# Another place for half of the inner sums of a two-level Strassen attention block, and an earlier time for some of them

## The chip, the cores and the metric

The kernel runs on one core of one Trainium2 chip. The metric is the device time of one execution in microseconds, the median of three runs. Lower is better. All data is fp32.

The engines have short names in the profile: PE is TensorE's matmul and PEld its weight load, DVE is VectorE, ACT is ScalarE, POOL is GpSimd (here almost only an issuer of DMAs), and SP is SyncE (the same).

## The reference

An image is 512 channels by 1024 positions; there are 16. Each is group-normalised, projected to q, k and v, attended in four heads of 128 channels, projected back and added to the input.

```python
xn  = groupnorm(x)                                   # (16, 512, 1024), 8 groups
qkv = einsum('oc,bcn->bon', qkv_w, xn) + qkv_b       # 1536 x 512 weights
q, k, v = split(qkv)                                 # four heads of 128
attn = softmax(einsum('bhnd,bhmd->bhnm', q, k) / sqrt(128))
out  = einsum('bhnm,bhmd->bhnd', attn, v)
out  = einsum('oc,bcn->bon', proj_w, out) + proj_b
return x + out
```

## The kernel before

The four projections of an image (first pair of heads' q and k, second pair's, v, and the output projection) are each made by Strassen's method on two levels: seven outer products, in four groups of two, two, two and one (`OUTER`), and in each group seven inner products (`ORDER`). For an outer product the inner level needs four inner sums of the right-hand operand, t1 to t4. VectorE makes them.

```python
OUTER = ((1, 5), (2, 6), (7, 4), (3,))
ORDER = (1, 2, 6, 5, 7, 4, 3)
```

The products are dealt out as units between the matmuls of attention, which run through everything: in each of eight steps of a head there are two score products (`s`, line 741) with their exponentials on ScalarE, and two of the weighted sum (`po`, line 836). The stages of image b are staggered against those of image b + 1:

```python
def plan_head(b, h):
    # h == 0: second pair's q and k of image b; sums of o of image b - 1
    # h == 1: output projection of image b - 1; load and normalise x of image b + 1
    # h == 2: first pair's q and k of image b + 1
    # h == 3: v of image b + 1
```

One function makes all four. Cuts are marked with "# ...".

```python
def two_levels(name, site, b, blocks, finish, sums="make"):
    R = {}
    haves = [{} for _ in OUTER]
    # ...
    def group_units(g):
        # ...
        def sum_tile(h, m):
            haves[h][m] = tpool.tile([P, 2, Q], F32, tag=f"in_{m}", name=f"{name}_{h}_{m}")
            return haves[h][m][:, : len(OUTER[h])]

        def load(h, m):
            if sums == "load" and h < len(OUTER):
                nc.sync.dma_start(sum_tile(h, m), inner_kept[b, h, m])

        def inner_sum(m):
            if sums == "load":
                return
            sum_tile(g, m)
            a, c = {"t1": ("b12", "b11"), "t2": ("b22", "t1"),
                    "t3": ("t2", "b11"), "t4": ("b21", "t2")}[m]
            for i in range(n):
                nc.vector.tensor_sub(have[m][:, i, :], inner(i, a), inner(i, c))   # L522
            if sums == "keep":
                t = dpool.tile([P, n, Q], F32, tag=f"{m}_{g}", bufs=1, name=f"kept_{m}_{g}")
                inner_kept[b, g, m] = t
                nc.gpsimd.dma_start(t, have[m][:, :n])                             # L526
        # ...
        return [
            unit(weights, lambda: inner_sum("t1"), lambda: inner_sum("t2"), p1),
            unit(lambda: inner_sum("t3"), p2), unit(lambda: inner_sum("t4"), p6),
            unit(lambda: load(g + 1, "t2"), p5), unit(lambda: load(g + 1, "t1"), p7),
            unit(lambda: load(g + 1, "t3"), p4),
            unit(lambda: load(g + 1, "t4"), p3, end),
        ]
```

The pool of `in_t1` to `in_t4` has one buffer for each name. So a group's t1 may be written only after the matmuls of the group before it have read theirs and, where the sums are kept, after the store of theirs has landed. The first pair keeps its sums in DRAM (`"keep"`); v of the same image loads them again (`"load"`); the second pair makes them anew (`"make"`), and so does the output projection.

Products gather in two banks of PSUM per name, x and y. An accumulator is evicted between additions: x by copies on ScalarE (line 448), y by additions on VectorE (line 557, into `r`), and the next product for that bank waits for the eviction.

The outer sums of o (the operand of the output projection) lie in six tiles of their own, `ot20` to `ot41`. Their values are made in head 0 at the latest and read in head 1:

```python
def sums_of_b(b, rows=(1, 2), chunks=range(KC)):       # L277: b["t2"], b["t3"], b["t4"]
    # ...
plan[6].append(lambda: o_blocks(b - 1))                # head 0, step 6
plan[6].append(lambda: sums_of_b(ob[b - 1]))
```

The output projection adds the residual x when a result is finished:

```python
def proj_groups(b):
    def finish(which, r, a, c):
        # ...
        t = ypool.tile([P, HALF], F32, tag="y", name=f"y_{b}_{o}_{half}")   # four buffers
        dma = nc.gpsimd.dma_start(t, x[b, ts(o, P), ts(half, HALF)])        # L712
        # ... not before the last eviction of this image's attention
        nc.vector.scalar_tensor_tensor(t, a, projb_sb[:, o : o + 1], t, ALU.add, ALU.add)  # L721
        nc.vector.tensor_add(t, t, c)                                       # L724
        nc.gpsimd.dma_start(out[b, ts(o, P), ts(half, HALF)], t)            # L725
```

v's results are transposed in blocks by VectorE (line 680), go to DRAM and come back into v's layout. The denominators of a finished head are a transpose and a reduction on VectorE (lines 763 and 765) and some small operations.

Each engine runs its queue in order. The order in which a queue's instructions stand is set when the kernel is built, by a scheduler that works from dependencies, and not by the source text alone.

Of the kernel before, what the change touches and what calls it, by code (L numbers as in the profile page):

```python
# [16 lines left out]
P = 128  # L17
# [4 lines left out]
HALF = 512  # L22
# [137 lines left out]
def fast_path(ctx, tc, x, sources, out, consts, flag, dims):  # L160
# [320 lines left out]
        units = {1: p1, 2: p2, 3: p3, 4: p4, 5: p5, 6: p6, 7: p7}  # L481
        return [units[i] for i in ORDER]

    def two_levels(name, site, b, blocks, finish, sums="make"):

# [3 lines left out]
        def part(g, i, row=None):  # L491
            t = R[g][:, i]
            return t if row is None else t[:, row, :]

        def group_units(g):
            group = OUTER[g]
            n = len(group)
            have = haves[g]

            def weights():  # L500
                have["w"] = group_weights(site, g, b == 0 and site in range(PAIRS))

            def sum_tile(h, m):
                haves[h][m] = tpool.tile(
                    [P, 2, Q], F32, tag=f"in_{m}", name=f"{name}_{h}_{m}"
                )
                return haves[h][m][:, : len(OUTER[h])]

            def load(h, m):
                if sums == "load" and h < len(OUTER):  # L510
                    nc.sync.dma_start(sum_tile(h, m), inner_kept[b, h, m])

            def inner_sum(m):
                if sums == "load":
                    return
                sum_tile(g, m)
                a, c = {
                    "t1": ("b12", "b11"), "t2": ("b22", "t1"), "t3": ("t2", "b11"),
                    "t4": ("b21", "t2"),
                }[m]  # L520
                for i in range(n):
                    nc.vector.tensor_sub(have[m][:, i, :], inner(i, a), inner(i, c))  # L522
                if sums == "keep":
                    t = dpool.tile([P, n, Q], F32, tag=f"{m}_{g}", bufs=1, name=f"kept_{m}_{g}")
                    inner_kept[b, g, m] = t
                    nc.gpsimd.dma_start(t, have[m][:, :n])  # L526

            def inner(i, m):
                if m[0] == "t":
                    return have[m][:, i, :]  # L530
                outer = blocks()[FACTORS[group[i]][1]]
                return outer[int(m[1]) - 1][:, ts(int(m[2]) - 1, Q)]

            def mm(acc, j, first):
                an, bn = FACTORS[j]
                t, slot = SLOTS[an]
                for i in range(n):
                    nc.tensor.matmul(  # L538
                        acc[:, ts(i, Q)], have["w"][t][:, i, slot, :], inner(i, bn),
                        start=(first and i == 0), stop=True, skip_group_check=True,  # L540
                    )

            def out_(which, a, c=None):
                row, half = int(which[1]) - 1, int(which[2]) - 1
                if g not in R:
                    R[g] = rpool.tile(
                        [P, 2, 2, HALF], F32, tag=f"r{g % 3}", name=f"{name}_r{g}"
                    )
                dst = R[g][:, :n, row, ts(half, Q)]

                def view(t):
                    return t[:, : n * Q].rearrange("p (i q) -> p i q", q=Q)

                if c is None:
                    nc.scalar.copy(dst, view(a))
                else:
                    nc.vector.tensor_add(dst, view(a), view(c))  # L557

            p1, p2, p6, p5, p7, p4, p3 = strassen(f"{name}_{g}", mm, out_, n * Q)

            def unit(*steps):
                def one():
                    for f in steps:
                        f()
                    for _ in range(min(len(pending), 2 if g == len(OUTER) - 1 else 1)):
                        pending.pop(0)()
                return one

            def end():
                combine(g)  # L570
                if g == len(OUTER) - 1:
                    run(pending)
                    pending.clear()


            return [
                unit(weights, lambda: inner_sum("t1"), lambda: inner_sum("t2"), p1),
                unit(lambda: inner_sum("t3"), p2), unit(lambda: inner_sum("t4"), p6),
                unit(lambda: load(g + 1, "t2"), p5), unit(lambda: load(g + 1, "t1"), p7),
                unit(lambda: load(g + 1, "t3"), p4),  # L580
                unit(lambda: load(g + 1, "t4"), p3, end),
            ]

        def first_loads():
            for m in ("t2", "t1", "t3", "t4"):
                t = tpool.tile([P, 2, Q], F32, tag=f"in_{m}", name=f"{name}_0_{m}")
                haves[0][m] = t
                nc.sync.dma_start(t, inner_kept[b, 0, m])

        pending = []  # L590

# [18 lines left out]
            elif g == 3:  # L610
                done("c12", (1, 0), (3, 0))

        ahead[name] = first_loads
        return [group_units(g) for g in range(len(OUTER))]


    def qk_groups(b, pair):

        def finish(which, r, a, c):
# [7 lines left out]
            )  # L627

        return two_levels(
            f"qk_{b}_{pair}", pair, b, lambda: xb[b], finish, "make" if pair else "keep"  # L630
        )

    def v_units(b, jj):
# [31 lines left out]
    def v_groups(b):  # L665
# [31 lines left out]
                    rows[which].rearrange("(k m) (q e) -> q m k e", m=BLK, q=n)[q],  # L697
                )

        return two_levels(f"v_{b}", "v", b, lambda: xb[b], finish, "load")  # L700

    def v_block(b, h, j):
        v, n = vs[b, h // 2], NB // NH2
# [1 line left out]

    def proj_groups(b):

        def finish(which, r, a, c):
            of, half = int(which[1]) - 1, int(which[2]) - 1
            o = 2 * of + r  # L710
            t = ypool.tile([P, HALF], F32, tag="y", name=f"y_{b}_{o}_{half}")
            dma = nc.gpsimd.dma_start(t, x[b, ts(o, P), ts(half, HALF)])  # L712

            tc.add_manual_dep(
                dma.ins, last_eviction[b].ins.name,
                mybir.DependencyInfo(
                    mybir.DependencyClass.Sync, mybir.DependencyReason.DATA
                ),
                reason="residual",
            )  # L720
            nc.vector.scalar_tensor_tensor(  # L721
                t, a, projb_sb[:, o : o + 1], t, ALU.add, ALU.add
            )
            nc.vector.tensor_add(t, t, c)  # L724
            nc.gpsimd.dma_start(out[b, ts(o, P), ts(half, HALF)], t)  # L725

        return two_levels(f"pp_{b}", "proj", b, lambda: ob[b], finish)


    ps, tot, po, rinv, last_eviction = {}, {}, {}, {}, {}  # L730
# [246 lines left out]
    def plan_head(b, h):  # L977
# [41 lines left out]
        else:  # L1019

            spread(plan, staggered(next_v.pop()), 0, NB - 1)
        return plan

    def warm(n, name):
# [24 lines left out]
    stage_sums(0)  # L1049
    run(staggered(qk_groups(0, 0)))  # L1050
    next_v, next_qk = [], [qk_groups(0, 1)]
    stage_blocks(1)
    stage_sums(1)

    plan = []
    for s in range(steps + 1):
        units = []
        if s < steps:
# [1 line left out]
            if j == 0:  # L1060
                plan = plan_head(b, h)
            units = plan[j]
            if j == NB - 1 and h > 1 and b + 1 < B:
                (next_v if h == 2 else next_qk).append(
                    v_groups(b + 1) if h == 2 else qk_groups(b + 1, 1)
                )
                if h == 2:
                    units.append(ahead[f"v_{b + 1}"])
        if 0 < s < steps and s % NB == 0:
            denominators(*where(s - 1)[:2])  # L1070
        for half in range(NH2):
# [148 lines left out]
```

## Time and profile before

| | |
|---|---|
| time, median of 3 runs | 3300.77 us (3296.75 to 3302.75) |
| span of the profiled execution | 3293.0 us |
| PE busy | 3198.6 us, 97% |
| DVE busy | 2639.3 us, 80% |
| ACT busy | 1443.6 us, 44% |
| inner sums on DVE, line 522, 128x256 | about 0.41 us each |
| store of a group's inner sum, from issue to landing | 3.5 us (256 KB, median) |
| load of a residual tile | 4.0 us (256 KB, median) |

A listed matmul overlaps the next one, so the sum of busy time overstates how full TensorE is: the distance from start to start tells more. The view of waits names, for each idle stretch of an engine, the instruction whose end released it; the timeline shows the same in square brackets behind the instruction that waited. An idle stretch of an engine that is not the bound costs nothing by itself.

### The profile page before, as it was taken

How to read it: one execution, taken by the hardware profiler on the slowest of the kernel's cores; microseconds unless marked ns; L12 is line 12 of the kernel's file. 1: busy time of each engine (PE TensorE's matmuls, PEld its weight loads, DVE VectorE, ACT ScalarE, POOL GpSimd, SP SyncE). 2: the span in 40 equal slices, each digit the busy share in tenths (PEclk: the TensorE clock that was granted, in tenths of full speed). 3: DMA queues.
4: the chain of work that ended last, by engine and by line, in shares of the span. 5: the costliest groups of instructions: out<-in, count | busy, mean ns of one | idle time of the engine just before them, and what ended most of it. 6: DMA issues, size and time to landing. Idle time of an engine off the chain costs nothing.

```text
span 3293.0 us, 34096 instructions
## 1 busy us (share of the span) xinstructions
PE 3198.6 (97%) x10474; PEld 2177.7 (66%) x10474; DVE 2639.3 (80%) x4625; ACT 1443.6 (44%) x2709; POOL 525.1 (16%) x938
## 2 busy tenths in 40 slices
PE   8999999999999999999999999999999999999999
PEld 6566666666666666666666666666666666666664
DVE  8878878778787787878888787887878878788684
ACT  2535435344353443534435354353533535344342
POOL 1011121111211112111121201212012120121100
PEclk9999999999999999999999999999999999999999
DMA  6554554545545455454554545546455463554631
GB/s 206 196 189 152 168 182 139 181 137 178 169 150 174 140 170 166 155 169 142 179 168 156 172 130 183 169 148 182 132 174 172 147 200 124 176 160 154 195 122 40
DMA packets 210539, 530.59 MB, mean 161 GB/s; under 512 B 33072, under 2 KB 66096, under 8 KB 210352
## 3 DMA queue, kind: packets, MB, share of 16 engines
q1 hardware_dynamic: 128992, 276.88, 27.2%
q0 software_dynamic: 67392, 216.07, 20.0%
q10 hardware_dynamic: 13968, 35.41, 3.1%
q8 instruction: 87, 1.43, 0.2%
q14 instruction: 100, 0.82, 0.1%
HBM read 389.56 MB, written 138.67 MB: 160 GB/s over the span
## 4 chain that ended last, share of the span: by engine, by line
issue 38%; PE 37%; DVE 11%; DMA 7%; POOL 5%; ACT 0%; POOLq 0%; SPq 0%; DVEq 0%
PE po L836 10%; PE s L741 10%; PE qk_x L538 5%; DMA vd<-vu 4%; POOL kept_t L526 4%; PE qk_y L538 4%; PE pp_x L538 4%; PE pp_y L538 3%; DMA out_y<-y 2%; DVE xt L277 2%; DMA y<-in_x 1%; DVE tot L754 1%; DVE vu L680 1%; DVE part L765 1%; DVE tt L763 1%
## 5 line engine op out<-in xcount | busy, mean ns | idle before, releaser
L836 PE MATMUL po<-p,v 128*128 128x512 f32 x2048 | 1056.6, 598 | 0.0
L741 PE MATMUL s<-qk,qk 128*128 128x512 f32 x2048 | 1052.8, 596 | 3.3 <-ACT p L746 3.2
L746 ACT ACTIVATE p<-s 128x512 f32<-128x512 f32 x1024 | 609.7, 596 | 851.6 <-PE s L741 810.0
L836 PEld LDWEIGHTS po<-p,v 128*128 128x128 f32 x2048 | 603.2, 303 | 328.2 <-issue 209.0
L754 DVE TENSOR_TENSOR tot<-tot,p 128x1024 f32<-128x1024 f32 x385 | 468.5, 1217 | 164.6 <-ACT p L746 162.6
L741 PEld LDWEIGHTS s<-qk,qk 128*128 128x128 f32 x2048 | 388.6, 191 | 106.4 <-issue 40.0
L538 PE MATMUL qk_x<-qk_t,w 128*128 128x256 f32 x1344 | 363.2, 387 | 43.0 <-DVE qk_t L522 38.6
L538 PEld LDWEIGHTS qk_x<-qk_t,w 128*128 128x128 f32 x1344 | 248.5, 191 | 211.9 <-issue 106.5
L448 ACT COPY qk_u<-qk_x 128x512 f32<-128x512 f32 (+1 forms) x256 | 136.1, 532 | 333.7 <-PE qk_x L538 286.7
L526 POOL DMA_DIRECT2D kept_t<-qk_t x256 | 138.3, 540 | 505.6 <-DVE qk_t L522 455.9
L688 POOL DMA_DIRECT2D vd<-vu x120 | 66.2, 552 | 747.5 <-DVE vu L680 745.8
L557 DVE TENSOR_TENSOR qk_r<-qk_y,qk_u 128x512 f32<-128x512 f32 (+1 forms) x256 | 158.3, 618 | 25.8 <-ACT qk_u L448 19.7
L538 PE MATMUL pp_x<-pp_t,w_proj 128*128 128x256 f32 x630 | 170.7, 387 | 6.4 <-ACT pp_p L448 6.4
L538 PE MATMUL v_x<-v_t,w_v 128*128 128x256 f32 x630 | 166.6, 381 | 0.0
L725 POOL DMA_DIRECT2D out_y<-y x120 | 66.2, 552 | 624.2 <-DVE y L724 591.6
L557 DVE TENSOR_TENSOR v_r<-v_y,v_u 128x512 f32<-128x512 f32 (+1 forms) x120 | 74.5, 621 | 112.5 <-ACT v_u L448 82.3
L538 PEld LDWEIGHTS pp_x<-pp_t,w_proj 128*128 128x128 f32 x630 | 113.9, 190 | 76.3 <-issue 22.5
L538 PEld LDWEIGHTS v_x<-v_t,w_v 128*128 128x128 f32 x630 | 118.5, 190 | 53.6 <-issue 23.0
L538 PE MATMUL qk_y<-x,w 128*128 128x256 f32 x512 | 144.4, 384 | 9.4 <-DVE qk_r L557 9.3
L693 POOL DMA_DIRECT2D v<-vd x240 | 139.9, 590 | 79.3 <-issue 67.1
L752 DVE TENSOR_TENSOR tot<-p,p 128x1024 f32<-128x1024 f32 x64 | 78.3, 1223 | 78.4 <-ACT p L746 78.4
L448 ACT COPY v_u<-v_x 128x512 f32<-128x512 f32 (+1 forms) x124 | 66.2, 534 | 165.1 <-PE v_x L538 126.2
(204 smaller groups left out, 4524.8 us busy)
## 6 DMA issues: line engine op xcount, KB each, us to landing
kept_t<-qk_t POOLq DMA_DIRECT2D x192, 256.0 KB, 3.5
w<-kept SPq DMA_DIRECT2D x90, 512.0 KB, 4.0
v_t<-kept_t SPq DMA_DIRECT2D x180, 256.0 KB, 3.0
w<-kept SPq DMA_DIRECT2D x90, 384.0 KB, 3.8
rinv<-row ACTq DMA_DIRECT2D x63, 512.0 KB, 5.5
x<-in_x POOLq DMA_DIRECT2D x60, 512.0 KB, 4.9
vd<-vu POOLq DMA_DIRECT2D x120, 256.0 KB, 3.4
v<-vd POOLq DMA_DIRECT2D x240, 128.0 KB, 4.5
```

The costliest lines, as they stand in the source:

```text
L448: nc.scalar.copy(t[n][:, :width], t["x"][:, :width])
L526: nc.gpsimd.dma_start(t, have[m][:, :n])
L538: nc.tensor.matmul(acc[:, ts(i, Q)], have["w"][t][:, i, slot, :], inner(i, bn), start=(first and i == 0), stop=True, skip_group_check=True,)
L557: nc.vector.tensor_add(dst, view(a), view(c))
L688: nc.gpsimd.dma_start(rows[which][ts(h, P), :], u)
L693: nc.gpsimd.dma_start(vs[b, pair][ts(q, BLK), half].rearrange("m h (k i) j -> m (h k) (i j)", k=n), rows[which].rearrange("(k m) (q e) -> ...
L725: nc.gpsimd.dma_start(out[b, ts(o, P), ts(half, HALF)], t)
L741: nc.tensor.matmul(sc, ks[b, h][:, ts(j, P)], qs[b, h][:, ts(half, HALF)], start=True, stop=True)
L746: nc.scalar.activation(ps[s][:, ts(half, HALF)], sc, AF.Exp, scale=SCALE)
L752: nc.vector.tensor_add(tot[b, h], ps[s - 1], ps[s])
L754: added[b, h, j] = nc.vector.tensor_add(tot[b, h][:, i], tot[b, h][:, i], ps[s][:, i])
L836: nc.tensor.matmul(po[b, h][:, i], v_block(b, h, j), ps[s][:, i], start=(j == 0), stop=(j == NB - 1),)
```

## The change

It has three parts.

1. Groups get one of two homes for their inner sums. Home B is the tiles from before, `in_t1` to `in_t4`. Home A is four of the tiles of o's outer sums: t1 and t2 in `ot20` and `ot21`, t3 and t4 in `ot30` and `ot31`. They are free from the end of the output projection until o's next outer sums. The first pair (from the second image on) and v alternate, "ABAB"; the second pair has "ABBB"; the output projection, whose operand lies there, stays "BBBB". A load now goes ahead to the next group of the same home, and v's second group is loaded when its first begins.
2. The second pair's units are prepared already at the end of head 2 of the image before, and the four inner sums of its first group are made in step 6 of that image's head 3 and no longer in its own first units. For the first image that happens ahead of the attention. The first image no longer stores its first pair's sums, which nothing loads.
3. The residual of a result is loaded when the fourth unit of the group that completes it begins (`prepare`), and not when the result is finished.

No work is added or taken out otherwise; the arithmetic is the same.

```diff
-    def two_levels(name, site, b, blocks, finish, sums="make"):
+    def two_levels(name, site, b, blocks, finish, sums="make", homes="BBBB", prepare=None):
 ...
+        def sum_tile(g, m):
+            k = int(m[1]) - 1
+            tag = f"in_{m}" if homes[g] == "B" else f"ot{2 + k // 2}{k % 2}"
+            t = tpool.tile([P, HALF], F32, tag=tag, name=f"{name}_{g}_{m}")
 ...
-            def load(h, m):
-                if sums == "load" and h < len(OUTER):
+            def load(m):
+                h = homes.find(homes[g], g + 1)
+                if sums == "load" and h > 0:
                     nc.sync.dma_start(sum_tile(h, m), inner_kept[b, h, m])
 
             def inner_sum(m):
 ...
+                if sums != "load" and m not in have:
+                    make_sum(g, m)
 ...
             return [
-                unit(weights, lambda: inner_sum("t1"), lambda: inner_sum("t2"), p1),
+                unit(
+                    weights, lambda: first_sums((1,)) if g == 0 and sums == "load" else None,
+                    lambda: inner_sum("t1"), lambda: inner_sum("t2"), p1,
+                ),
                 unit(lambda: inner_sum("t3"), p2), unit(lambda: inner_sum("t4"), p6),
-                unit(lambda: load(g + 1, "t2"), p5), unit(lambda: load(g + 1, "t1"), p7),
 ...
+                unit(lambda: load("t2"), lambda: ready(g), p5), unit(lambda: load("t1"), p7),
+                unit(lambda: load("t3"), p4), unit(lambda: load("t4"), p3, end),
             ]
 ...
+        def first_sums(groups=(0,)):
+            for g in groups:
+                for m in ("t1", "t2", "t3", "t4"):
+                    if sums == "load":
+                        nc.sync.dma_start(sum_tile(g, m), inner_kept[b, g, m])
+                    else:
+                        make_sum(g, m)
+
+        results = {1: ("c11",), 2: ("c22", "c21"), 3: ("c12",)}
+
+        def ready(g):
+            for which in results.get(g, ()) if prepare else ():
+                for r in range(2):
+                    prepare(which, r)
 ...
-            f"qk_{b}_{pair}", pair, b, lambda: xb[b], finish, "make" if pair else "keep"
+            f"qk_{b}_{pair}", pair, b, lambda: xb[b], finish,
+            "make" if pair or b == 0 else "keep",
+            "ABBB" if pair else "ABAB" if b > 0 else "BBBB",
 ...
-        return two_levels(f"v_{b}", "v", b, lambda: xb[b], finish, "load")
+        return two_levels(f"v_{b}", "v", b, lambda: xb[b], finish, "load", "ABAB")
 ...
+        def prepare(which, r):
+            o, half = place(which, r)
+            t = ys[which, r] = ypool.tile([P, HALF], F32, tag="y", name=f"y_{b}_{o}_{half}")
             dma = nc.gpsimd.dma_start(t, x[b, ts(o, P), ts(half, HALF)])
 ...
             spread(plan, staggered(next_v.pop()), 0, NB - 1)
+
+            plan[NB - 2].append(lambda: ahead[f"qk_{b + 1}_1"]())
 ...
     next_v, next_qk = [], [qk_groups(0, 1)]
+    ahead["qk_0_1"]()
 ...
-            if j == NB - 1 and h > 1 and b + 1 < B:
-                (next_v if h == 2 else next_qk).append(
-                    v_groups(b + 1) if h == 2 else qk_groups(b + 1, 1)
-                )
-                if h == 2:
-                    units.append(ahead[f"v_{b + 1}"])
+            if j == NB - 1 and h == 2 and b + 1 < B:
+                next_v.append(v_groups(b + 1))
+                next_qk.append(qk_groups(b + 1, 1))
+                units.append(ahead[f"v_{b + 1}"])
```

## The prediction

> **What bounds the kernel now.** I read the page's busy table first, then who TensorE waited for, then the two timelines around the longest wait.
>
> ```profile
> PE 3198.6 (97%) x10474; PEld 2177.7 (66%) x10474; DVE 2639.3 (80%) x4625; ACT 1443.6 (44%) x2709; POOL 525.1 (16%) x938
> ```
>
> TensorE (PE) is the bound, but 97% is not what is left to win. In the timeline a pair of 128x512 matmuls is listed at 1.02 us, yet the next pair starts 0.86 us later: 0.43 us per 512 columns, 0.215 per 256. Adding up over the whole timeline how much later each matmul starts than that after the one before gives 144 us. No change that only removes waits brings more than 144 of the 3293.
>
> PE's waits, in us in total, times and longest:
>
> ```profile
> PE qk_x L538 <- DVE qk_t L522: 38.6, 30, 2.8
> PE qk_y L538 <- DVE qk_r L557: 9.6, 14, 2.4
> PE v_y L538 <- DVE v_r L557: 9.1, 15, 0.6
> ```
>
> The first line is the inner sums (qk_t). Of its 30 waits 15 are over 2 us, one in each image after the first, always where the image's first head begins. Around one of them, PE and then DVE:
>
> ```profile
> 1477.56 1.02 PE L741 MATMUL s<-qk,qk 128*128 128x512 f32 x2
> 1478.42 1.02 PE L836 MATMUL po<-p,v 128*128 128x512 f32 x2
> 1479.28 1.03 PE L538 MATMUL qk_y<-qk_t,w 128*128 128x256 f32 x4
> 1482.61 1.48 PE L538 MATMUL qk_x<-qk_t,w 128*128 128x256 f32 x4 [2.31 <-DVE qk_t L522]
> 1483.92 1.02 PE L741 MATMUL s<-qk,qk 128*128 128x512 f32 x2
> ```
>
> ```profile
> 1478.93 1.23 DVE L763 STREAM_TRANSPOSE tt<-tot 128x1024 f32<-128x1024 f32 x1
> 1480.07 1.05 DVE L680 STREAM_TRANSPOSE vu<-vt 128x512 f32<-128x512 f32 x1
> 1480.96 1.17 DVE L765 TENSOR_REDUCE part<-tt 128x32 f32<-128x1024 f32 x1
> 1482.04 0.42 DVE L522 TENSOR_TENSOR qk_t<-x,qk_t 128x256 f32<-128x256 f32 x1
> ```
>
> The reader is to see that DVE is not waiting: t2 merely stands behind the transposes of v and the last head's denominators. PE should start the four qk_x at 1480.14 (1479.28 + 0.86) and starts at 1482.61: 2.47 us lost. Then it runs at the pace of DVE's halves of t2 (1.31 us to the next start for 0.86): 0.45 more. Sum 2.92 us per image. In some images the granted clock falls too (span, busy PE, PEld, DVE, ACT, POOL, clock, DMA share, GB/s):
>
> ```profile
> 1279.00:1283.80 4.80, 4.70 (x9) 2.18 (x10) 4.42 (x17) 1.18 (x2) 4.49 (x8) 0.64 0.84 203
> 1482.60:1487.40 4.80, 4.68 (x17) 3.32 (x18) 4.75 (x19) 1.77 (x3) 4.12 (x8) 1.00 0.85 214
> ```
>
> Over 4.8 us a mean of 0.64 is about 3.4 us at half clock, so 1.7 us lost. Six of the 15 stretches after the wait are like that (0.64 to 0.68), nine have 1.00.
>
> [...] here a gap of 2.3 us was enough in six cases of 15. So removing the gap should remove the slow stretch. [...] the long gap is one of order on DVE, and the buffers (one tile per inner sum) are what forbids another order. [...] The trace has 416 to 418 for most inner sums, but back to back they start 0.335 us apart, and that is what I use.
>
> **Part 1, the second pair's first four sums (8 subtractions) move into head four.** The built order of instructions shows it: on DVE all eight now stand before the tail of v, and PE's order differs only in trifles (t2's product stands before t1's; one product of v stands before the one that waits). What it removes is the wait: 15 x 2.92 = 44 us, plus 6 x 1.7 = 10 us of low clock, **54 us**. But does DVE have room? The first 24 us of head four do (11.33 of 24.30 us busy in 1220.70 to 1245.00), but the sums are not put there. They stand in 1250 to 1283, where DVE is busy 32.39 of 33.00 us. DVE's total does not fall, so this is the risk. I count the new order from the old starts. The eight sums add 8 x 0.335 = 2.7 us; three outer sums of o (L277), whose tiles are now taken, go behind group 0 into the next head and take away 1.9; two subtractions slip into gaps ahead of a transpose that waited for its input, 0.3. So v's last evictions come 0.5 us later. PE's product of v that needs one of them started at 1267.32, as the add ended: it should now wait up to 0.5. Against that, the product moved ahead (0.43 us) fills part of the other wait on v_r (0.61 before L538 at 1257.73), and I take off 0.3. Net about +0.2 x 15 = **3 us lost**. After that the head begins with group 0's sums ready. The next thing PE needs from DVE is the eviction of group 0's fifth product, before its last product may add to that bank: In the built order PE comes to that 16 slots of 0.86 us (a pair of s, of po, or four 256-wide ones) after its first qk_x (1272.16 before, 1272.7 with the delay), at 1286.5. DVE, with l, group 1's sums and the two moved outer sums in front, has it at about 1285.0. A margin of 1.5 us: thin, but a margin.
>
> **Part 2, alternate groups in o's tiles (t1 and t2 in ot2, t3 and t4 in ot3).** Group 1 no longer has to wait until group 0's matmuls have read its sums and, where the sums are kept for v, until the store has landed. Where that ended last it is dear:
>
> ```profile
> 1187.41 0.43 DVE L522 TENSOR_TENSOR qk_t<-qk_t,x 128x256 f32<-128x256 f32 x1 [2.31 <-DMA kept_t<-qk_t]
> ...
> 1188.49 2.07 PE L538 MATMUL qk_y<-x,w 128*128 128x256 f32 x4 [2.44 <-DVE qk_r L557]
> ```
>
> But this is one image. In most of them the first quarter of head three loses about 2.0 us, with DVE busy nearly without a break (denominators, x's outer sums, then the inner sums), and DVE's order there is the same in both kernels until group 2. Summed by image, only two stand out above 2.0, by 1.4 and 3.4 us: **5 us** gained, and 0.2 us x 15 = 3 us where DVE waited for PE's reading. For v the homes change only loads, and no PE wait names a v load: 0. For the first image the stores are dropped; its sums also stand earlier in the prologue: 0, give or take 2.
>
> **Part 3, the residual.** It is asked for earlier in the source, but the order on POOL's queue is the same before and after, with the same waits: the last two loads still need the tiles of the first results of group 2, whose stores must land first. So VectorE's wait, in the same view, stays, and I count 0:
>
> ```profile
> DVE y L721 <- DMA y<-in_x: 18.6, 20, 1.3
> ```
>
> **Sum.** 54 - 3 + 5 + 3 = 59 us if all goes through. I take 53, because 54 supposes that no DVE-paced rest and no low clock remain anywhere: 3300.77 - 53 = **3248 us**, 1.6% less.
>
> **Rivals.** (a) DVE becomes the bound between 1250 and 1285: the wait only moves, from t2 to an eviction (qk_r or v_r) a few us later. For it: DVE 98% busy there, its work not reduced, and the thin margin. Against it: the slack of later results, and 3.1 us of DVE work that PE does not need at once (the last two adds of v at 0.6 and transposes at 0.95). It would leave a wait of 1 to 2 us per image: 15 to 30 us given back, 3265 to 3278. (b) The store landing matters more than I think, and head three's 2.0 us vanish as well: 15 x 2 = 30 more, 3220 to 3225. Against it: in those images the bracket names no store, and DVE's queue is full. (c) The borrowed tiles bring a wait of their own: o's outer sums must wait until group 0's t1 and t3 are read, and stand in DVE's queue ahead of the eviction. t3 is read by about 1280.5 and DVE arrives at about 1283.7, so I expect nothing; if PE were later, DVE and PE would wait in turn and part of the 54 would go, to about 3265.
>
> **Range and chances.** The low end, 3234, is the plan with all 59 us and part of (b); the high end, 3268, is (a) in its mild form. Faster by over 2% means below 3234.8 and needs (b): 0.10. Slower by over 2% would need a stall of 8 us per image, and nothing in the order shows one: 0.01. Within 2%: 0.89.
>
> **What would show it.** Right: the wait of qk_x on qk_t falls from 38.6 us to under 6 with none over 1 us; the stretches of clock below 1 go from seven in the body to one or two; POOL's y loads are as before; head three still loses about 2 us per image. Wrong: PE waits on qk_r or v_r by over 10 us more than now (rival a), or head three's waits go (rival b), or the wait of DVE on y falls (part 3).

## The result, and the profile after

| | before | changed |
|---|---|---|
| time, median | 3301.76 us (3296.75 to 3303.72, 4 runs) | 3248.01 us (3241.69 to 3253.53, 4 runs) |
| ratio to before | | 0.984, 95% interval [0.982, 0.986] |
| span of the profiled execution | 3293.0 us | 3251.7 us |

The change makes the kernel 1.6% faster, and the predicted 3248 us is what was measured. That the two agree to the microsecond is luck: the four runs of the changed kernel lie between 3241.69 and 3253.53 us. The experiments below show that the sum was right for reasons that were partly wrong: its main term is no property of the part to which it was given.

The busy line of the changed kernel's page: the work is the same, the span shorter.

```profile
PE 3185.4 (98%) x10474; PEld 2178.0 (67%) x10474; DVE 2633.3 (81%) x4625; ACT 1439.8 (44%) x2709; POOL 516.3 (16%) x922
```

Lines have moved: L548, L518, L567 and L777 of the changed kernel are L538, L522, L557 and L746 of the kernel before. PE's waits in the changed kernel (us in total, times, longest):

```profile
PE v_y L548 <- DVE v_r L567: 13.7, 30, 0.7
...
PE qk_y L548 <- DVE qk_t L518: 8.5, 14, 1.3
...
PE s L772 <- ACT p L777: 4.3, 6, 2.3
PE qk_x L548 <- DVE qk_t L518: 3.5, 15, 1.2
```

In the kernel before, two of these were:

```profile
PE qk_y L538 <- DVE qk_t L522: 3.5, 10, 1.3
PE s L741 <- ACT p L746: 3.2, 2, 2.3
```

The wait of qk_x on qk_t was 38.6 us with 15 stretches over 2 us and is 3.5, the longest 1.2. The wait of qk_y on qk_r (9.6) is 0.4. Other waits grew: qk_y on qk_t from 3.5 to 8.5 (4.9 in kernel 2 below, which is nearly the same program), v_y on v_r from 9.1 to 13.7, and PE's wait on ScalarE's p from 3.2 to 4.3. The last looks like a trifle and turns out to be the key to experiments 5 to 7.

The same place as in the prediction, an image's first head, on PE and then the stretch of DVE ahead of it:

```profile
1257.12 1.03 PE L548 MATMUL qk_y<-x,w 128*128 128x256 f32 x4
1257.98 1.02 PE L772 MATMUL s<-qk,qk 128*128 128x512 f32 x2
1258.84 1.02 PE L867 MATMUL po<-p,v 128*128 128x512 f32 x2
1259.70 1.03 PE L548 MATMUL qk_x<-qk_t,w 128*128 128x256 f32 x4
1260.56 1.03 PE L548 MATMUL qk_y<-qk_t,w 128*128 128x256 f32 x4
1261.43 1.02 PE L772 MATMUL s<-qk,qk 128*128 128x512 f32 x2
```

```profile
1246.84 0.45 DVE L518 TENSOR_TENSOR qk_t<-x,qk_t 128x256 f32<-128x256 f32 x1
1247.17 1.12 DVE L703 STREAM_TRANSPOSE vu<-vt 128x512 f32<-128x512 f32 x1
...
1254.80 0.46 DVE L567 TENSOR_TENSOR v_r<-v_y,v_u 128x256 f32<-128x256 f32 x1
1255.13 1.26 DVE L785 TENSOR_TENSOR tot<-tot,p 128x1024 f32<-128x1024 f32 x1
1256.25 0.73 DVE L700 TENSOR_TENSOR vt<-v_r,v_r 128x512 f32<-128x512 f32 x1
1256.85 1.29 DVE L794 STREAM_TRANSPOSE tt<-tot 128x1024 f32<-128x1024 f32 x1
```

On PE every start follows the last by 0.86 us, though each group is listed at 1.02 or 1.03. On DVE the last of group 0's sums stands at 1246.84, 10 us ahead of the transpose tt; before, t2 stood behind tt and its reduction.

To compare kernels I use the sum of the prediction: how much later than 0.43 us per 512 columns (0.215 per 256) each matmul starts after the one before, added up over the timeline and split by place. All these kernels run the same matmuls, so span less this sum is nearly one number by construction (3148 to 3150 us in the fourteen profiles): the sum says where a difference lies, not why. Each row comes from one profiled execution; kernel 2 and the changed kernel, nearly one program, differ by up to 5 us in a column and by 10 in the total. Heads one to four are `h == 0` to `h == 3` of the plan. Parts are numbered as in the prediction: part one is the second pair's first sums, part two the homes, part three the residual. The two stretches of head one are its first two steps and its rest; "head four" is its second half with the prologue; heads two, the rest of three and the rest of four (22 to 25 us in all) are left out but counted in the total. The ratio is to the kernel before, timed on the same chip; the kernel before took 3296.7 us beside kernels 1, 2, 3 and 5, 3297.3 beside 4, 6, 8 and 10, and 3305.4 beside 7, 9, 11 and 12.

| kernel | time, us | ratio, 95% interval | head one, start | head one, rest | head three, first half | head four | total lost, us |
|---|---|---|---|---|---|---|---|
| before | 3301.8 | | 54.3 | 4.9 | 37.6 | 24.0 | 144.5 |
| changed | 3248.0 | 0.984 [0.982, 0.986] | 0.7 | 9.3 | 35.7 | 32.4 | 101.8 |
| 1: part one alone | 3299.1 | 1.0005 [0.9996, 1.0015] | 11.7 | 25.9 | 52.3 | 27.8 | 141.3 |
| 2: no early request | 3244.6 | 0.984 [0.983, 0.986] | 1.1 | 5.7 | 30.4 | 31.1 | 91.9 |
| 3: request, old tiles | 3243.5 | 0.984 [0.983, 0.985] | 1.7 | 9.6 | 30.3 | 25.2 | 90.4 |
| 4: neither | 3279.8 | 0.994 [0.992, 0.996] | 47.5 | 4.6 | 33.9 | 24.0 | 133.6 |
| 5: v in home B | 3274.2 | 0.993 [0.991, 0.994] | 11.5 | 31.8 | 30.6 | 27.5 | 124.6 |
| 6: 5, rows on SyncE | 3236.1 | 0.982 [0.980, 0.983] | 1.6 | 3.6 | 28.1 | 27.3 | 83.5 |
| 7: changed, rows on SyncE | 3237.8 | 0.980 [0.978, 0.982] | 1.2 | 3.8 | 27.3 | 29.8 | 86.4 |
| 8: first pair in home B | 3279.0 | 0.995 [0.993, 0.997] | 1.1 | 6.7 | 63.4 | 31.8 | 126.7 |
| 9: 8, v as BABA | 3257.0 | 0.985 [0.983, 0.987] | 0.5 | 3.5 | 47.7 | 31.1 | 106.7 |
| 10: spare half for c12 | 3223.5 | 0.978 [0.976, 0.979] | 1.3 | 5.3 | 7.9 | 31.0 | 68.6 |
| 11: 3, rows, spare half | 3218.4 | 0.974 [0.972, 0.976] | 2.6 | 6.9 | 9.8 | 23.6 | 66.4 |
| 12: 5, rows, spare half | 3215.4 | 0.973 [0.971, 0.975] | 1.8 | 2.7 | 9.1 | 27.6 | 63.5 |

### The profile page after: what moved, and what is told of

Same layout as the page of the kernel before. It is cut to its first block, busy times and chain, and to the rows that moved or that the text cites. A ratio compares the mean times of both kernels' runs of the same rounds, so it can differ in the third digit from the quotient of the medians.

```text
span 3251.7 us, 34056 instructions
## 1 busy us (share of the span) xinstructions
PE 3185.4 (98%) x10474; PEld 2178.0 (67%) x10474; DVE 2633.3 (81%) x4625; ACT 1439.8 (44%) x2709; POOL 516.3 (16%) x922
## 3 DMA queue, kind: packets, MB, share of 16 engines
q1 hardware_dynamic: 128992, 276.88, 27.5%
## 4 chain that ended last, share of the span: by engine, by line
PE 47%; issue 27%; DVE 16%; DMA 7%; POOL 2%; ACT 1%; ACTq 0%; POOLq 0%; SPq 0%; DVEq 0%
PE po L867 13%; PE s L772 13%; PE qk_x L548 6%; PE qk_y L548 5%; PE pp_x L548 4%; DVE qk_t L518 3%; PE pp_y L548 3%; DMA vd<-vu 2%; DVE xt L277 2%; DMA out_y<-y 2%; DMA y<-in_x 2%; DMA v<-vd 1%; DVE qk_r L567 1%; DVE vu L703 1%; DVE tot L785 1%
## 5 line engine op out<-in xcount | busy, mean ns | idle before, releaser
L777 ACT ACTIVATE p<-s 128x512 f32<-128x512 f32 x1024 | 610.0, 596 | 895.9 <-PE s L772 817.1
L548 PE MATMUL qk_x<-qk_t,w 128*128 128x256 f32 x1344 | 356.8, 384 | 9.4 <-DVE qk_t L518 3.5
L548 PEld LDWEIGHTS qk_x<-qk_t,w 128*128 128x128 f32 x1344 | 250.2, 190 | 170.0 <-issue 66.2
L567 DVE TENSOR_TENSOR qk_r<-qk_y,qk_u 128x512 f32<-128x512 f32 (+1 forms) x256 | 158.3, 619 | 40.1 <-ACT qk_u L448 26.3
L548 PE MATMUL pp_x<-pp_t,w_proj 128*128 128x256 f32 x630 | 170.8, 388 | 6.7 <-ACT pp_p L448 6.7
L567 DVE TENSOR_TENSOR v_r<-v_y,v_u 128x512 f32<-128x512 f32 (+1 forms) x120 | 76.5, 638 | 112.2 <-ACT v_u L448 82.0
L548 PE MATMUL v_x<-v_t,w_v 128*128 128x256 f32 x630 | 166.7, 381 | 0.0
L522 POOL DMA_DIRECT2D kept_t<-qk_t x240 | 129.2, 540 | 233.4 <-DVE qk_t L518 188.7
L548 PEld LDWEIGHTS pp_x<-pp_t,w_proj 128*128 128x128 f32 x630 | 114.0, 190 | 76.4 <-issue 22.5
L548 PEld LDWEIGHTS v_x<-v_t,w_v 128*128 128x128 f32 x630 | 118.6, 190 | 55.2 <-issue 19.1
L548 PE MATMUL qk_y<-x,w 128*128 128x256 f32 x512 | 143.5, 382 | 0.0
L646 DVE SCALAR_TENSOR_TENSOR qk<-qk_r,qkb_sb,qk_r 128x512 f32<-128x512 f32 x192 | 137.3, 743 | 1.6
```

The costliest lines, as they stand in the source:

```text
L522: nc.gpsimd.dma_start(t, to)
L548: nc.tensor.matmul(acc[:, ts(i, Q)], have["w"][t][:, i, slot, :], inner(i, bn), start=(first and i == 0), stop=True, skip_group_check=True,)
L646: nc.vector.scalar_tensor_tensor(st[b, h][:, ts(half, HALF)], a, qkb_sb[:, i : i + 1], c, ALU.add, ALU.add)
L777: nc.scalar.activation(ps[s][:, ts(half, HALF)], sc, AF.Exp, scale=SCALE)
```

## The experiments

### What removes the wait at the start of head one: 1 to 4

**1. Part one alone.** The other homes and the early residual are undone.

```diff
-            "ABBB" if pair else "ABAB" if b > 0 else "BBBB",
+            "ABBB" if pair else "BBBB",
 ...
-    return two_levels(f"v_{b}", "v", b, lambda: xb[b], finish, "load", "ABAB")
+    return two_levels(f"v_{b}", "v", b, lambda: xb[b], finish, "load")
 ...
             o, half = place(which, r)
+            prepare(which, r)
             t = ys.pop((which, r))
 ...
-        return two_levels(f"pp_{b}", "proj", b, lambda: ob[b], finish, prepare=prepare)
+        return two_levels(f"pp_{b}", "proj", b, lambda: ob[b], finish)
```

> The second pair's first sums alone: no other stage has tiles of o as a home, and the residual is loaded at the finish as before. My theory (the gain is the removed stand-still of PE at the start of head one, 53.6 us of lost time in the traces) expects about 3245 us, with the wait of PE on qk_t below 8 us in total. Rival, the homes of the first pair and v bring a good part of it: then 3270 or more. Since the tiles of o are free all through the third and fourth head in this kernel, the eight sums also stand earlier in VectorE's order, in the fourth head's first half or before, so the losses at the end of the fourth head should be those of the kernel before (about 17 us without the prologue) and not those of the changed one (24): that would make it some 5 us faster than the changed kernel, not slower.

Measured: no gain at all, ratio 1.0005 [0.9996, 1.0015]. The wait on qk_t went as expected, and others came. PE's waits in this kernel:

```profile
PE s L773 <- ACT p L778: 22.1, 13, 3.2
PE qk_y L548 <- DVE qk_r L567: 17.4, 15, 2.8
...
PE qk_x L548 <- ACT qk_u L448: 7.8, 16, 1.0
...
PE qk_x L548 <- DVE qk_t L518: 3.5, 15, 1.2
```

So my theory, that the removed wait is the gain, falls in this form: the same 43 us left the start of head one, 21 came back in the rest of it and 15 in head three. The built order says why they are not where they are in the changed kernel: with o's tiles free so early, all eight sums stand in head three, among the first pair's own. The loss in head one is the one that kernel 5 shows below, with waits on ScalarE's p and qk_u of the same size; that in head three comes back at kernel 8.

**2. The changed kernel without the early request.**

```diff
-            plan[NB - 2].append(lambda: ahead[f"qk_{b + 1}_1"]())
 ...
-    ahead["qk_0_1"]()
```

> The changed kernel without part one: homes and residual stay, and the second pair's first sums are made in its own first units again. My theory expects the wait of PE on qk_t back at about 38 us with 15 waits over 2 us, the low clock after some of them too, and a time of 3293 to 3300 us (only the few us of part two remain). Rival, the homes of alternate groups bring the gain: 3255 to 3270 us.

Measured: 0.984, as the changed kernel. The expectation was wrong by 50 us. The built orders show why: on DVE, ScalarE, POOL and SyncE this kernel is the changed one, instruction by instruction, and on PE one product of po per image stands elsewhere. Given tiles that are free, the scheduler moved the sums ahead without being asked. (So the 3.4 us between the two times are what two measurements of nearly one program differ by.)

**3. The request without the tiles.**

```diff
-            "ABBB" if pair else "ABAB" if b > 0 else "BBBB",
+            "BBBB" if pair else "ABAB" if b > 0 else "BBBB",
```

> The second pair's first sums are asked for as early as in the changed kernel, but their tiles are in_t1 to in_t4 (home B), which v's fourth group holds until its matmuls have read them. In the built order the eight sums then stand amid the tail of v, behind its last evictions. If the homes are what makes the early sums possible, PE's wait on qk_t or on v_r returns in part: 1 to 2 us per image, 3265 to 3285 us. If the time of asking were enough and the tiles only a detail: 3248, as the changed kernel.

Measured: 0.984 again. The sums stand later here, all but the first behind v's last eviction, yet ahead of tt, and that is early enough; v's own wait on v_r is back at 9.2 us.

**4. Neither** (the edits of 2 and 3 together).

> The first pair and v alternate homes as in the changed kernel, but the second pair has its old tiles and its sums are asked for in its own first units. The changed kernel without the early request was as fast as with it, and so was the one with the request and the old tiles. If the two are two ways to the same order on VectorE (the sums ahead of the transposes and the denominators), then with neither the wait on qk_t comes back with 35 us or more and the time is 3285 to 3300. Rival, the alternate homes of v and of the first pair bring the gain by themselves: 3245 to 3260.

Measured: 0.994 [0.992, 0.996], a little below the range. PE's wait is back:

```profile
PE qk_x L548 <- DVE qk_t L518: 35.2, 30, 2.5
```

What follows from the four: the request and the tiles are two ways to have these sums ahead of tt on DVE, and either is enough, if v and the first pair have their alternate homes (an early request without any new home was not run). Removing both loses 46 us at the start of head one. What is left in kernel 4, the alternate homes of v and the first pair with the earlier residual, brings 0.6%.

### ScalarE, which nobody had counted: 5 to 7

**5. v all in home B, the rest as changed.**

```diff
-    return two_levels(f"v_{b}", "v", b, lambda: xb[b], finish, "load", "ABAB")
+    return two_levels(f"v_{b}", "v", b, lambda: xb[b], finish, "load")
```

> The changed kernel with v's groups all in home B. The tiles of o are then free earlier, and the built order has the second pair's eight sums in the fourth head's middle, where VectorE has idle time, and not among v's last evictions. My theory, that the changed kernel loses about 7 us more than the one before at the end of the fourth head because these eight sums stand ahead of v's evictions, expects this loss gone and perhaps more (v's own wait, 9 us before): 3233 to 3242 us. Rival, that loss is the noise of the counting or has another cause, or v's alternate homes bring something of their own: 3248 or more.

Measured: slower than the changed kernel, 0.993 against 0.984. The 5 us at the end of head four came as expected (32.4 to 27.5), and 33 us were lost in head one. The eight sums stand in the last three steps of head three in this trace, not in the middle of head four. PE's waits on ScalarE have grown (4.3 and 2.2 us in the changed kernel):

```profile
PE s L772 <- ACT p L777: 22.0, 12, 2.5
PE qk_x L548 <- ACT qk_u L448: 7.6, 16, 1.0
```

The timelines of this kernel's ScalarE, and of PE at the same time:

```profile
1273.20 0.32 ACTq L816 DMA_DIRECT2D row<-r  x1
1273.62 0.60 ACT L777 ACTIVATE p<-s 128x512 f32<-128x512 f32 x1 [4.62 <-PE s L772]
1274.12 0.58 ACT L448 COPY qk_u<-qk_x 128x512 f32<-128x512 f32 x1
1279.07 0.33 ACTq L821 DMA_DIRECT2D rinv<-row  x1
1279.44 0.59 ACT L448 COPY qk_p<-qk_x 128x512 f32<-128x512 f32 x1 [4.74 <-PE qk_y L548]
1279.92 0.60 ACT L777 ACTIVATE p<-s 128x512 f32<-128x512 f32 x1
```

```profile
1278.30 1.03 PE L548 MATMUL qk_y<-x,w 128*128 128x256 f32 x4
1280.58 1.13 PE L772 MATMUL s<-qk,qk 128*128 128x512 f32 x2 [1.25 <-ACT p L777]
```

ScalarE's queue holds two transfers of the finished head's reciprocal denominators: row<-r to DRAM, and rinv<-row back to all partitions, which may be issued only when the first has landed. Between 1274.70 and 1279.07 ScalarE does nothing. The bracket names PE's qk_y; it is not the cause, since ScalarE's copy reads qk_x and not that bank. The cause is the issue of rinv<-row. It is listed for 0.33 us only, but it opens 5.87 us after row<-r was issued, and row<-r took 5.9 us to its landing (this kernel's DMA view, 1270 to 1282): ScalarE stood in that wait for 4.37 us. What is built behind such an issue did not pass it. In the trace of the changed kernel ScalarE's 2588 activations and copies start in built order without an exception, and none ahead of a transfer issue that was built before it; nor is there an exception among PE's 10474 matmuls, 4512 operations of DVE, 916 of POOL and SyncE's 846 issues. Only the other way round is there one: 15 of ScalarE's 139 issues are listed ahead of one or two operations built before them, by up to 0.9 us. Meanwhile scores wait for their exponentials, and the next s has no bank to write to. The images of this kernel differ, and bear it out: in the 14 from the second on, the four in which row<-r landed after 2.9 to 4.3 us lose 0.15 us each in the rest of head one, the ten in which it took 5.4 to 7.0 us lose 1.2 to 4.4.

The changed kernel has the same pair, with the landing named, in its timeline of ScalarE:

```profile
1264.09 0.33 ACTq L816 DMA_DIRECT2D row<-r  x1
...
1269.40 0.33 ACTq L821 DMA_DIRECT2D rinv<-row  x1
1269.77 0.58 ACT L448 COPY qk_p<-qk_x 128x512 f32<-128x512 f32 x1 [4.18 <-DMA row<-r]
1270.25 0.60 ACT L777 ACTIVATE p<-s 128x512 f32<-128x512 f32 x1
```

PE's s comes at 1270.90 there, just without a wait. In kernel 5 row<-r goes out 11.1 us after the head's first s (mean of 14 images), in the changed one 9.6: between v's last eviction and the last addition into tot its DVE has five other operations, and the changed kernel's has none (as its fence above shows). In the kernel before, PE had stood waiting for t2 and did not come to this point early.

**6. Kernel 5 with the two transfers on SyncE.**

```diff
-            nc.scalar.dma_start(
+            nc.sync.dma_start(
                 row.rearrange("o (c i) -> (o c) i", i=BLK), inverse.pop((b, h))
 ...
-        nc.scalar.dma_start(rinv[b, h], rows_of.pop((b, h)).to_broadcast((P, N)))
+        nc.sync.dma_start(rinv[b, h], rows_of.pop((b, h)).to_broadcast((P, N)))
```

> The kernel with v all in home B (3274 us), with one more edit: the two transfers that carry the reciprocal denominators of a finished head (row<-r and rinv<-row) are issued from SyncE's queue and not from ScalarE's. My new theory: with the wait at the start of head one gone, PE runs into ScalarE, which stands some 4 us between these two issues because the second waits for the first to land; in the traces that costs 12 + 32 us of lost PE time in head one. If that is so, the waits of PE on ScalarE's p and qk_u in head one go and the time falls by 25 to 35 us, to 3240 to 3250. Rival: ScalarE is late because VectorE is (its additions into qk_r and the inner sums come late in any case): then PE's wait only changes its name and the time stays above 3265.

Measured: 3236.1 us, 38 less and better than expected. The queue of SyncE and then ScalarE, in this kernel's timeline:

```profile
1256.12 0.32 SPq L816 DMA_DIRECT2D row<-r  x1
1261.19 0.32 SPq L821 DMA_DIRECT2D rinv<-row  x1
```

```profile
1258.27 0.59 ACT L565 COPY qk_r<-qk_x 128x512 f32<-128x512 f32 x1 [1.12 <-PE qk_x L548]
1259.13 0.60 ACT L777 ACTIVATE p<-s 128x512 f32<-128x512 f32 x1 [0.27 <-PE s L772]
```

The transfers take as long as before (5.1 us between the issues here; on average of 14 images 5.75, in kernel 5 5.55), but ScalarE now works in between. Head one loses 5 us in all, where it lost 43. In head one the order on PE, on VectorE and, these two issues apart, on ScalarE is the same in kernels 5 and 6. That VectorE was late in any case, the rival, is ruled out.

The choice of the issuing engine was worth 38 us here: what it freed was not the 0.33 us for which an issue is listed but the wait ahead of it (4.37 us in kernel 5's fence).

**7. The same edit on the changed kernel.**

> The changed kernel with the two transfers of the denominators issued from SyncE's queue. In head one after its first two steps it loses 9.3 us of PE time, mostly waits on ScalarE's p. The same edit took 38 us off the kernel with v in home B. My theory expects the loss in that part of head one to fall to about 4 us and the time by about 5: 3240 to 3246. Rival, in the changed kernel these waits have another cause or the edit brings something else too: no gain, or over 10 us.

Measured: 3237.8 us, 10 less by the times and 14 by the ratios (0.980 [0.978, 0.982] against 0.984 [0.982, 0.986]): more than the 5 expected, and the size that I had given to the rival. Head one's rest fell from 9.3 to 3.8 us, as expected, but kernel 2 has 5.7 there without this edit, so 2 to 5.5 us are the edit's. With the transfers on SyncE each of the 14 images from the second on loses 0.15 us in this stretch; in the changed kernel they lose 0.16 to 1.09. Another 8 us went in head three. Kernels 2 and 3 lose 5 us less there without this edit, and the edit changes the order on PE and DVE there: how much of it is the edit's is not shown.

### The homes of the first pair: 8 and 9

**8. The first pair in home B, the rest as changed.**

```diff
-            "ABBB" if pair else "ABAB" if b > 0 else "BBBB",
+            "ABBB" if pair else "BBBB",
```

> The changed kernel with the first pair's groups all in home B again. The prediction gave the alternate homes of the first pair 5 us + 3 us. If so: about 3250 to 3258. The kernel with part one alone lost 15 us more in the first half of head three than the kernel before; if that came from the missing homes of the first pair and not from sums that were hoisted into head three, this kernel loses them too and takes 3265 or more. If the homes of the first pair are worth nothing: 3248 or less.

Measured: 3279.0 us. The first half of head three loses 27.7 us more than in the changed kernel with no sums hoisted into it: in this kernel's built order the second pair's sums stand in head four. So the missing homes are enough for a loss. (Kernel 1's 15 us are not settled by this, since v has home B there.) PE's largest wait, and DVE's:

```profile
PE qk_y L548 <- DVE qk_r L567: 27.8, 15, 3.6
```

```profile
DVE qk_t L518 <- DMA kept_t<-qk_t: 36.7, 29, 3.5
```

That is the store's landing that the prediction looked for in the kernel before and found dear in two images. There it was, in all:

```profile
DVE qk_t L522 <- DMA kept_t<-qk_t: 10.8, 17, 2.3
```

The DMA view of ten microseconds around one such wait shows what is new:

```profile
kept_t<-qk_t POOLq DMA_DIRECT2D x6, 256.0 KB, 5.8
w<-kept SPq DMA_DIRECT2D x1, 512.0 KB, 4.2
v_t<-kept_t SPq DMA_DIRECT2D x2, 256.0 KB, 6.0
```

v's first group has o's tiles as its home. When the first pair does not use these, v's loads go out in the third step of head three, beside the stores that DVE is waiting for. The store of group 0's t3 landed after 5.4 us (mean of 14 images), against 4.1 in the kernel before, where no v_t runs at this time. Not all of this is v's loads: in the changed kernel and in kernel 1 none runs at this time either, and the store took 4.7. Loads issued from SyncE run beside stores issued from POOL in this fence, and both are slower: a v_t of 256 KB took 6.0 us (3.0 as the median of the kernel before), a kept_t of 256 KB 5.8 (3.5 there).

**9. Kernel 8 with v's homes in the other order,** so that v's first group waits for the first pair's tiles.

```diff
-    return two_levels(f"v_{b}", "v", b, lambda: xb[b], finish, "load", "ABAB")
+    return two_levels(f"v_{b}", "v", b, lambda: xb[b], finish, "load", "BABA")
```

> The kernel with the first pair in home B (3279 us), with v's homes in the other order, BABA. In that kernel v's first group could be loaded into the tiles of o some 15 us after the start of head three, and in the trace those loads run beside the store of t3 that VectorE waits for: it landed after about 5.2 us, in the kernel before after about 4.1. With BABA v's first group has to wait for the first pair's tiles, as before. If the collision is the cause, the store lands after about 4 us again, VectorE's wait on kept_t falls from 36.7 us to 10 to 15, PE's on qk_r from 27.8 to about 10, and the time is 3250 to 3262. Rival: the store waits for the first pair's tiles are what the loss is, with or without v's loads: 3270 or more.

Measured: 3257.0 us, as expected, but the waits fell less than I had said: DVE's on kept_t from 36.7 to 28.8, PE's on qk_r from 27.8 to 16.5, and the store lands after 4.6 us, not 4.1. So the time of v's loads explains the larger part of the distance between kernel 8 and the changed one: 20 of 25 us by the lost starts in all, 15.7 of 27.7 in the first half of head three. The new order does not clear head three of v's loads: its second group has o's tiles as its home now, and these four loads go out in the third to fifth step. That may be what keeps DVE's wait so long; no run tells. The 4.6 us of the store are near the changed kernel's 4.7; why both are half a microsecond above the kernel before stays open.

### What was left in head three: 10, and two sums: 11 and 12

**10. The last residual pair in a tile of its own.** The fourth group has one outer product, so half of R[3] is unused.

```diff
-                    prepare(which, r)
+                    prepare(which, r, R[3][:, 1, r, :] if g == 3 else None)
 ...
-        def prepare(which, r):
+        def prepare(which, r, t=None):
-            t = ys[which, r] = ypool.tile([P, HALF], F32, tag="y", name=f"y_{b}_{o}_{half}")
+            if t is None:
+                t = ypool.tile([P, HALF], F32, tag="y", name=f"y_{b}_{o}_{half}")
+            ys[which, r] = t
```

> The changed kernel, but the last residual pair (c12) is loaded into the half of R[3] that nothing uses, so that its load need not wait until an earlier result of the four-tile ring has been stored. My theory: the load's issue waits for that store's landing (POOL waits 99.5 us on out_y, VectorE 26.4 us on y in the changed kernel), and the late addition holds VectorE in front of head three's outer and inner sums. Then the wait on y falls below 5 us, the first half of head three loses 10 to 20 us less, and the time is 3228 to 3240. Rival: VectorE is full there anyway, and only the name of its wait changes: 3245 to 3250.

Measured: 3223.5 us, ratio 0.978 [0.976, 0.979]: a little more than expected. The changed kernel's view of DVE's waits has

```profile
DVE y L752 <- DMA y<-in_x: 26.4, 18, 2.2
```

and kernel 10 has no such line, only one for the new tile:

```profile
DVE pp_r L754 <- DMA pp_r<-in_x: 1.1, 1, 1.1
```

The first half of head three loses 7.9 us, not 35.7; in 12 of the 14 images from the second on exactly 0.24. The rival, that DVE is full there and only the name of its wait would change, falls.

**11 and 12. Together.** Kernel 11 is kernel 3 with the edits of 6 and 10, kernel 12 is kernel 5 with them.

> A candidate: the changed kernel with the second pair back in its old tiles (early request kept, 3243 us alone), the last residual pair in the unused half of R[3] (25 us less), and the denominators' transfers on SyncE. If the three add up: 3243.5 - 25 - 6 = about 3213 us. If the removed waits share one cause or VectorE becomes the bound in their place: 3220 or more.

> The other candidate: v all in home B, denominators' transfers on SyncE (3236 us together), and the last residual pair in the unused half of R[3]. If the gains add up: 3236 - 25 = about 3211 us, with the first half of head three losing about 8 us of PE time and not 28. If not: 3225 or more.

Measured: 3218.4 and 3215.4 us, both some 5 us above the plain sums (on a chip where the kernel before took 8 us more than in the runs that the sums are made of) and below the 3220 and 3225 named for the other case. Most of the gains add up. Kernel 12's busy line:

```profile
PE 3170.8 (99%) x10474; PEld 2179.2 (68%) x10474; DVE 2639.1 (82%) x4625; ACT 1442.4 (45%) x2709; POOL 516.2 (16%) x922
```

Of 144.5 lost microseconds 63.5 are left, a third of them in head two, which no experiment touched.

## Why the prediction was right, and where its reasons were not

The time, 3248 us, was right. Point by point:

- **The bound: right as far as it was tried.** Kernel 12 took back 81.0 of the 144.5 us of lost starts, and its span is 80.7 shorter. That span less lost starts is about 3149 us in all kernels is no proof, since all run the same matmuls.
- **Part 1, 54 us: the size was right, the owner was not.** The start of head one lost 54.3 us and loses 0.7; the slow clock went too (ahead of the last microseconds the kernel before has eight stretches of half clock, 0.50 for 3.41 us each, one in the first image and six behind this wait; the changed kernel has one, in the first image at 170.8. The prediction counted seven. Kernel 4, where the wait is back, has four behind it. Why a stretch follows six of the 15 waits and not the other nine is not shown). But part one alone brought nothing (kernel 1), and its early request was not needed (kernel 2). The sentence that failed is "the buffers (one tile per inner sum) are what forbids another order": kernel 3 has the old buffers for these sums and the better order (v and the first pair keep their new homes in it). The old order came from both at once, sums asked for late and tiles that come free late; either cure works.
- **The cost in head four, 3 us: mis-sized.** The second half of head four, without the prologue, went from 17.0 to 24.0 us: 7 lost. The v_y that waits on v_r starts 0.73 us late per image where the step had 0.5, and the product moved ahead gave 0.26 back, where 0.3 was counted. The margin at the fifth product's eviction, "thin, but a margin", held: PE's wait on qk_r is 0.4 us.
- **Missing: ScalarE.** The step looked for the next thing that PE needs from DVE and not at what DVE's denominators hold up on ScalarE's queue. It cost the changed kernel up to 4.4 us in head one's rest (0.8 in kernel 2), and kernel 5 33 us in head one. In the image shown the changed kernel passes that point with almost no margin.
- **Part 2, 5 + 3 us: right as a difference, wrong as an account.** The seven kernels that have the changed one's first-pair homes and residual lose 35.7, 30.4, 30.3, 33.9, 30.6, 28.1 and 27.3 us in this stretch, 30.9 on average, against 37.6: 7 gained. The two images that stand out, from which the step took its 5 us, did not go: the changed kernel has two again, of 4.1 and 4.4 us. What fell is the typical image, from 2.1 to 1.6 us (median of 14). And without the first pair's homes the changed kernel would lose 31 us, and "for v the homes change only loads, and no PE wait names a v load: 0" missed that these loads can delay a store (5.4 us to its landing in kernel 8, 4.6 in kernel 9), and that v's homes decide where the second pair's sums may stand (kernel 5: 26 us).
- **That head three still loses about 2 us per image: nearly right; its reason was wrong.** DVE is busy there, but it starts late, behind the last residual: with that load free, 25 us go (kernel 10). Rival (b) had nearly the size, 30 us, and another cause, the store of the sums.
- **Part 3, 0: right.** In the traces POOL's queue has the same order in the kernel before and the changed one, but for the stores that the first image no longer makes, and also in kernels 1 and 5, one with the residual loaded at the finish and one with it early. The changed kernel with this part alone undone was not run. DVE's wait on y did not fall (18.6 before, 26.4 now).
- **Rival (a)** came in a form not foreseen: not as an eviction, but as ScalarE waiting for DVE's denominators and for the landing of row<-r (5.5 us in head one). **Rival (c)** did not show: no wait of o's outer sums on t1 or t3.
- **The sum of 59, taken as 53,** came out at 53.8 by the times. The lost starts of the two profiled executions differ by 42.7: 53.6 at the start of head one, less 4.4 in its rest, plus 1.9 in head three, less 8.4 in head four. Their spans differ by 41.3, as the changed kernel's profile is of the slowest of its four runs; kernel 2 differs by 52.6. The 6 us taken off for rests happened to cover costs that were not foreseen, so the exact hit is luck. A term of a few us can't be read from one pair.

## What to carry to other kernels

A term that is read from a trace ("this wait costs 54 us") belongs to an order of instructions, not to the edit that is meant to bring it: undo each part alone before you credit it, and expect parts to be alternatives or to need one another. Before you take a wait away, ask what the engine that then arrives earlier will meet next, on every engine's queue, and look for transfers whose issue has to wait on a queue that also feeds the bound (4.37 us in kernel 5's fence). A load that is late because its tile is still being stored is cheap to free if any tile lies unused (25 us in kernel 10).

## What the runs showed of the hardware that I had not expected

The 4 KB transfer row<-r took 5.5 us from issue to landing in head one of the changed kernel (mean of 14, 5.1 to 6.1) and 2.4 us in head three. In head one of kernel 5 it took 2.9 and 3.2 us where the DMA engines were 0.62 and 0.68 busy (share in the profile, 2082.70 to 2085.63 and 467.00 to 470.20), and 6.9 and 7.0 us where the share was 1.04 and 0.96 (1474.10 to 1480.96 and 2886.70 to 2893.70). That it waits for the large transfers in flight is my reading of this, and is not shown. The prediction had not counted such a row at all.
